# Two LoRA layers on one core: the first weight product fed chunk by chunk, and half of a small product moved into the weight stage

## The chip, the core and the metric

The kernel runs on one core of a Trainium2 chip. The metric is the device time of one execution in microseconds (us). Before the change the median of three runs is 326.9 us (325.46 to 327.69).

## What is computed

Two residual layers follow one another, each with a dense weight and a low-rank part that an index per batch picks:

```python
# layer 0: x is 8 x 256 x 1024, W0 1024 x 1024, rank 32, scale 16/32
x = x + einsum('bsi,oi->bso', x, W0) + (einsum(x, lora_A0[idx0[b]]) @ lora_B0.T) * 0.5
# layer 1: W1 1024 x 1024, bias b, rank 16, scale 2
x = x + einsum('bti,oi->bto', x, W1) + b + (einsum(x, lora_A1[idx1[b]]) @ lora_B1[idx1[b]]) * 2
```

All in 32-bit floats. The residual is the identity added to the weight, so the dense part is x (I + W0)^T (I + W1)^T. The kernel multiplies the two weights first, into one matrix M, and then x by M.

## The kernel before

The engines are TensorE (PE), VectorE (DVE), ScalarE (ACT), GpSimd (POOL) and SyncE (SP), which issues most DMAs. The order of the work on each engine is the order of the program text, written out by hand (`manual_schedule`, L937); each engine runs its own instructions in that order and waits for the others by semaphores. DMAs of the hardware queues take turns on eight semaphores, so a DMA is issued only when the one eight before it has landed.

There are two stages. The weight stage (to about 115 us) forms M from W0 and W1 in halves of 512 columns and rows, by a scheme with seven block products in place of eight, at two levels. The x stage then takes the batches in four pairs. The change lies in the first 55 us of the weight stage:

- Loads (L943 to L956). `w1_rows` holds W1's first 256 rows, in two DMAs on SP and ACT. Then SP loads W0's chunks k = 0 to 3 of the first column half (`load_w0`, L173; 128 x 512, 256 KB each), the second half of W1's first block (`load_w1`, L163, four DMAs of 128 KB), the block W1[0,1] (four of 256 KB), W0's chunks 4 to 7, the small `b0`, and W1[1,0] and W1[1,1].
- Warm-up and turning (L960 to L986). PE multiplies the identity by itself, then turns the eight 128 x 128 squares of `w1_rows` into two PSUM banks. One DVE and one ACT copy bring them to `w1T` (L1021, L1022).
- First products (L1023 to L1032, `first`). The first block product P1 has four groups of rows, each in a PSUM bank of its own, and four chunks k. The columns 0 to 255 come first, with the identity added to W0 (`diag_w0`, L180) and to W1 (L1030) by DVE.
- Then `turn_w1` (L225) turns the other half of W1's first block on DVE, 32 x 32 squares at a time, and the columns 256 to 511 follow, group by group; ACT keeps each group's result (`keep_p1`, L294) and puts it back into PSUM as the start of other sums (`load_inner`).
- `load_a1` (L193) fetches the eight picked rank-16 matrices A1 by eight DMAs of 64 KB on POOL. A POOL copy from `m22` (L195) holds them until the first group is kept. POOL then copies each to its place in `a1` (L203).
- Four turnings of W1[0,1] on DVE; then the "second" block product (class `Second`, L609), which is itself a seven-product scheme: `products([1, 2])` for its two halves, then, after the sums of W1's quarters on DVE (`Second.op.sums`, L416 to L421), products 6, 5, 4, 7, 3 of each.
- `prepare_up` and `prepare_down` (L716, L744): small products for the low-rank parts. `prepare_down(h)` is half h of G = A1 times (I + W0): eight products of 128 x 512 over all eight chunks of W0's column half h, and one ACT copy. Before, both halves stand behind the second block product, after `prepare_up(h)`.
- Beside it DVE turns W1[1,0], adds up the second product (`form`, L584), turns W1[1,1], forms the sums of W1's blocks (`sums_w1_first`, L354; four calls of two) with the four `diag_w0` of chunks 4 to 7 among them, and the sums of W0 (`w_groups[0].sums`, L264). POOL adds the identity to W1[1,*] (L235). The product of L282 that follows ("product 6" of the first group) needs all of these but W0's last two sums.

Of the kernel before, what the change touches and what calls it, by code (L numbers as in the profile page):

```python
# [10 lines left out]
ALU = mybir.AluOpType  # L11
# [9 lines left out]
P = 128  # L21
# [3 lines left out]
MLOW = 64  # L25
BIAS = 48
NWARM = 6
# [6 lines left out]
NQ = NH // 2  # L34
NB = 4
# [6 lines left out]
def kernel(  # L42
# [37 lines left out]
    nc = tc.nc  # L80

    B, T, D = x.shape
    NJ = T // P
    NK = D // P
    NO = D // NH
    NR = NH // SQ
    N0, _, R0 = lora_a0.shape
    N1, _, R1 = lora_a1.shape
# [5 lines left out]
    ident = const.tile([P, P], F32, tag="ident", name="ident")  # L94
# [34 lines left out]
    def fix_indices(rawi, n: int, layer: int):  # L129
        wrap = const.tile([1, B], I32, tag=f"wrap{layer}", name=f"wrap{layer}")  # L130
        nc.vector.tensor_scalar(wrap, rawi, 0, n, ALU.is_lt, ALU.mult)
        fixed = const.tile([1, B], I32, tag=f"fixed{layer}", name=f"fixed{layer}")
        nc.vector.tensor_tensor(fixed, rawi, wrap, ALU.add)
        nc.vector.tensor_scalar(fixed, fixed, 0, n - 1, ALU.max, ALU.min)
        return fixed

    def index(fixed, b: int, n: int, engine=SP):
        return nc.values_load(
            fixed[0:1, b : b + 1],
            engines=[engine],  # L140
            min_val=0,
            max_val=n - 1,
            skip_runtime_bounds_check_because="clamped on the chip",
        )
# [14 lines left out]
    def new_w1(h: int, i: int):  # L159
        both = units[:, 4 * h + 2 * i : 4 * h + 2 * i + 2].rearrange("p u n -> p (u n)")  # L160
        return both.rearrange("p (t c) -> p t c", t=NR)

    def load_w1(wq, h: int, i: int, lo: int = 0, hi: int = NR):  # L163

        rows = slice(h * NH + lo * SQ, h * NH + hi * SQ)
        for g in range(NG):
            cols = slice(i * NH + g * P, i * NH + (g + 1) * P)
            nc.sync.dma_start(  # L168
                wq[g * SQ : (g + 1) * SQ, lo:hi, :],
                w1[rows, cols].rearrange("(t q) c -> q t c", q=SQ),  # L170
            )

    def load_w0(k: int, i: int):  # L173
        cols = slice(i * NH, (i + 1) * NH)
        rows = w0[(k // NB) * NH : (k // NB + 1) * NH, cols]
        nc.sync.dma_start(
            w0n[:, k, cols], rows.rearrange("(p m) c -> p m c", m=NB)[:, k % NB, :]
        )

    def diag_w0(k: int):  # L180
        diag = w0n[:, k].rearrange("p (i q m) -> p i m q", i=2, m=NB)[:, k // NB, k % NB]
        nc.vector.tensor_tensor(diag, diag, ident, ALU.add)

    def load_b0():
        nc.sync.dma_start(
            b0.rearrange("p (i m) r -> p i (m r)", i=2),
            lora_b0.rearrange("(i p m) r -> p i (m r)", i=2, m=NB),
        )
# [2 lines left out]
    a1_rows = work[:, 0 : 2 * NH].rearrange("p (b k r) -> p b k r", b=B, k=NK)  # L191

    def load_a1():  # L193

        nc.gpsimd.tensor_copy(a1_rows[0:1, 0, 0, 0:1], m22[0:1, 0, 0:1])  # L195
        for b in range(B):
            j = index(fixed1, b, N1, mybir.EngineType.Pool)
            nc.gpsimd.dma_start(
                a1_rows[:, b].rearrange("p (i m) r -> p i (m r)", m=NB),
                lora_a1[bass.ds(j, 1)].rearrange("o (i p m) r -> p (o i) (m r)", i=2, m=NB),  # L200
            )
        for b in range(B):
            nc.gpsimd.tensor_copy(a1[:, :, b, :], a1_rows[:, b])  # L203
# [45 lines left out]
    def new_bank():  # L249
        ring.append(ring.pop(0))  # L250
        return ring[-1]
# [102 lines left out]
    def sums_w1_first(k: int):  # L354
        nc.vector.tensor_tensor(tw[:, 1, k, :], w_b["22"](k), w1T[:, k, NH:D], ALU.subtract)
        nc.vector.tensor_tensor(tw[:, 0, k, :], tw[:, 1, k, :], w_b["11"](k), ALU.add)
# [277 lines left out]
    def load_inner(ps, tiles):  # L634

        p = m22[:, tiles, :].rearrange("p m (h n) -> p (m h) n", h=2)
        for i, part in ((2, 0), (4, 2), (5, 3)):
            nc.scalar.copy(slot(ps, i), p[:, part])
# [77 lines left out]
    def prepare_up(h: int):  # L716
        pm = new_bank()
        for k in range(NK):
            g = k % 4
            nc.tensor.matmul(  # L720
                pm[g * R0 : (g + 1) * R0, :],
                b0[:, k, :],
                w1T[:, k, h * NH : (h + 1) * NH],
                start=(k < 4),
                stop=(k >= NK - 4),
            )
        nc.scalar.copy(ups[1][:, h * NH : (h + 1) * NH], pm)
# [13 lines left out]

    gT = [work[:, (4 + h) * NH : (5 + h) * NH] for h in range(NO)]

    def prepare_down(h: int):  # L744
        pm = new_bank()
        for k in range(NK):
            nc.tensor.matmul(  # L747
                pm,
                a1[:, k].rearrange("p b r -> p (b r)"),
                w0n[:, k, h * NH : (h + 1) * NH],  # L750
                start=(k == 0),
                stop=(k == NK - 1),
            )
        nc.scalar.copy(gT[h], pm)
# [182 lines left out]
    with tc.manual_schedule(engines=ORDERED):  # L937
# [5 lines left out]
        w1_rows = units[:, 0].rearrange("p (t c) -> p t c", t=2)  # L943
        for t, engine in enumerate((nc.sync, nc.scalar)):
            engine.dma_start(w1_rows[:, t], w1[t * P : (t + 1) * P, 0:NH])
        for k in range(NB):
            load_w0(k, 0)
        load_w1(wq[0, 0], 0, 0, mid, NR)
        wq[0, 1] = new_w1(0, 1)
        load_w1(wq[0, 1], 0, 1)  # L950
        for k in range(NB, NK):
            load_w0(k, 0)
        load_b0()
        for i in range(2):
            wq[1, i] = new_w1(1, i)
            load_w1(wq[1, i], 1, i)  # L956
        nc.scalar.copy(s_all[:, 0:R0], ident[:, 0:R0])


        def warm_up(first, last):  # L960
            for n in range(first, last):
                bank, i = banks[6 + n // 4], n % 4
                nc.tensor.matmul(
                    bank[:, i * P : (i + 1) * P],
                    ident,
                    ident,
                    start=(i == 0),
                    stop=True,
                    skip_group_check=True,
                )  # L970

        warm_up(0, NWARM)
        w1_turned = [banks[4 + t].rearrange("p (m q) -> p m q", m=NB) for t in range(2)]
        for t in range(2):
            for m in range(NB):
                rows = w1_rows[:, t].rearrange("p (q m) -> p m q", m=NB)[:, m]
                nc.tensor.matmul(
                    w1_turned[t][:, m, :],
                    rows,
                    ident,  # L980
                    start=(m == 0),
                    stop=True,
                    is_transpose=True,
                    skip_group_check=True,
                )
        warm_up(4, 7)  # L986
        raw0, raw1 = load_indices(idx0, 0), load_indices(idx1, 1)
        nc.gpsimd.memset(scale, L1_SCALING)
        for half in range(2):
# [20 lines left out]
        def first(g, k: int, n: int):  # L1010
            cols = slice(n * NH // 2, (n + 1) * NH // 2)
            nc.tensor.matmul(  # L1012
                g.p1[:, cols],
                g.a[0][:, k, :],
                w1T[:, k, cols],
                start=False,
                stop=(k == NB - 1),
                skip_group_check=True,
            )

        nc.scalar.copy(w1T[:, 0:NB, P : 2 * P], w1_turned[1])  # L1021
        nc.vector.tensor_copy(w1T[:, 0:NB, 0:P], w1_turned[0])  # L1022
        for k in range(NB):  # L1023
            diag_w0(k)
            if k == 0:

                part = w1T[0:MLOW, 0, 0:1]
                diag = bass.AP(part.tensor, part.offset, [part.ap[0], [D + 1, NB], [NB, MLOW]])
                same = ident[0:MLOW, 0:MLOW].unsqueeze(1).to_broadcast([MLOW, NB, MLOW])
                nc.vector.tensor_tensor(diag, diag, same, ALU.add)  # L1030
            for g in w_groups:
                first(g, k, 0)  # L1032
        fixed0, fixed1 = fix_indices(raw0, N0, 0), fix_indices(raw1, N1, 1)
        for k in range(NB):
            turn_w1(wq[0, 0], 0, k, mid, NR)
        seconds = [Second(n) for n in range(2)]
        one, other = seconds
        zero_inner(one.ps)
        for m, g in enumerate(w_groups):
            for k in range(NB):  # L1040
                first(g, k, 1)
            g.keep_p1(m22[:, m, :])
            if m % 2:
                load_inner(seconds[m // 2].ps, seconds[m // 2].tiles)
        load_a1()
        for k in range(NB, NK):
            turn_w1(wq[0, 1], 0, k)
        one.products([1, 2])
# [12 lines left out]
        other.products([6, 5, 4, 7, 3])  # L1061
        keep(other.kept, other.ps)
        prepare_up(0)
        prepare_down(0)
        for k in range(NB):
            turn_w1(wq[1, 0], 1, k)
        one.form()
        for k in range(NB):
            turn_w1(wq[1, 1], 1, NB + k)
        for k in range(NB):  # L1070
            sums_w1_first(k)
            if k == 1:
                for n in range(NB, NK):
                    diag_w0(n)
        prepare_up(1)
        prepare_down(1)
        prepare_cross()
        w_groups[0].sums()
        sums_w1_last()
# [280 lines left out]
```

## Time and profile before

| What | us |
| --- | --- |
| median of three runs | 326.9 |
| the profiled execution | 325.97 |
| its span, first to last instruction | 323.9 |
| PE busy in the span | 317.9 (98%) |
| DVE busy in the span | 253.7 (78%) |
| PE's first product on weights | at 7.05 |
| PE's chain without gaps begins | at 15.77 |

The span is cut into stretches by the steps above. The columns are the busy time of each engine with its number of instructions, the granted clock of PE (1.00 is full), the mean share of the DMA engines' time (over 1 where packets overlap) and the rate.

```profile
0.00:7.05 7.05, 4.84 (x26) 4.54 (x26) 3.66 (x8) 2.09 (x3) 5.15 (x22) 1.00 0.68 230
7.05:15.77 8.72, 8.48 (x38) 7.34 (x39) 5.40 (x18) 0.00 (x0) 0.00 (x0) 1.00 1.22 187
15.77:24.99 9.22, 9.22 (x42) 8.08 (x43) 7.32 (x13) 4.12 (x10) 5.26 (x9) 1.00 1.17 219
24.99:34.00 9.01, 9.01 (x46) 7.72 (x48) 8.94 (x17) 1.84 (x4) 3.20 (x7) 1.00 1.19 174
34.00:53.02 19.02, 19.02 (x80) 7.18 (x80) 15.08 (x24) 4.06 (x8) 3.13 (x6) 1.00 0.70 174
53.02:120.00 66.98, 66.98 (x250) 42.91 (x247) 60.98 (x111) 14.89 (x31) 26.49 (x30) 1.00 0.73 127
```

In a line of a timeline the first number is the start, the second the time covered, then engine, source line, operation, tiles, count, and in brackets the idle time before it and what ended it. In the chain of waits a line is start, length and what the time went to.

### The profile page before, as it was taken

What the parts mean: (1) busy time and instruction counts of PE and PEld (TensorE: products, weight loads), DVE (VectorE), ACT (ScalarE), POOL (GpSimd) and SP (SyncE); (2) the same over time, 40 slices, a digit from 0 to 9 for tenths busy, and PEclk for the clock granted to TensorE, in tenths of its full rate; (3) what the DMA queues carried; (4) which work ended last, traced back from release to release, by engine and by line L of the source; (5) the groups of instructions that cost most, each with busy time, mean ns of one, the idle gap of its engine ahead of it and who ended that gap; (6) DMA issues with size and microseconds to landing.
All of it is one profiled execution on the core that took longest, in us unless ns stands there. A gap on an engine that the chain in (4) does not pass through costs nothing.

```text
span 323.9 us, 4417 instructions
## 1 busy us (share of the span) xinstructions
PE 317.9 (98%) x1494; PEld 247.0 (76%) x1494; DVE 253.7 (78%) x490; ACT 59.9 (18%) x125; POOL 70.1 (22%) x107
## 2 busy tenths in 40 slices
PE   7999999999999999999999999999999999999995
PEld 6888434444588878888878888878888878888884
DVE  5679599879999899999969686929775929632965
ACT  2052215000224223640010420000240000222000
POOL 6053232455132231671004000003100000000000
PEclk9999999999999999999999999999999999999999
DMA  7999954987264995796417610235630111100113
GB/s 223 188 227 171 267 127 78 170 139 152 56 100 85 193 165 95 112 172 108 129 68 187 153 34 0 92 104 146 156 74 0 65 67 65 65 2 0 66 67 130
DMA packets 64910, 36.42 MB, mean 112 GB/s; under 512 B 45508, under 2 KB 58932, under 8 KB 64888
## 3 DMA queue, kind: packets, MB, share of 16 engines
q1 hardware_dynamic: 56088, 20.87, 29.7%
q0 software_dynamic: 8656, 15.01, 22.5%
q8 instruction: 12, 0.20, 0.2%
q10 hardware_dynamic: 144, 0.26, 0.2%
q14 instruction: 10, 0.08, 0.1%
HBM read 19.02 MB, written 8.39 MB: 85 GB/s over the span
## 4 chain that ended last, share of the span: by engine, by line
PE 94%; DMA 3%; DVE 1%; issue 0%; SPq 0%; DVEq 0%
PE bank L527 71%; PE bank L282 11%; PE bank L797 4%; PE bank L747 4%; DMA units<-in_L_cond_W_dram 3%; PE bank L1012 2%; PE bank L720 1%; DVE w1T L227 1%; PE bank L815 1%; DVE w1T L235 0%; PE bank L761 0%; PE bank L547 0%; DVE work L885 0%; SPq L168 0%; DVEq L227 0%
## 5 line engine op out<-in xcount | busy, mean ns | idle before, releaser
L509 DVE TENSOR_TENSOR work<-bank,work 128x512 f32<-128x512 f32 (+1 forms) x56 | 32.1, 618 | 30.6 <-PE bank L527 15.4
L505 ACT COPY work<-bank 128x512 f32<-128x512 f32 (+1 forms) x60 | 27.6, 546 | 77.3 <-PE bank L527 52.2
L931 POOL DMA_DIRECT2D out_dram<-work x12 | 8.9, 743 | 115.8 <-DVE work L607 115.8
L240 DVE STREAM_TRANSPOSE units<-units 128x512 f32<-128x512 f32 x32 | 20.1, 680 | 6.8 <-DMA units<-in_x_dram 6.8
L527 PE MATMUL bank<-w0n,w1T 128*128 128x256 f32 x104 | 24.1, 379 | 0.0
L527 PE MATMUL bank<-w1T,s_all 128*128 128x256 f32 x88 | 22.3, 379 | 0.0
L527 PEld LDWEIGHTS bank<-w0n,w1T 128*128 128x128 f32 x104 | 19.8, 190 | 2.7
L527 PE MATMUL bank<-w0n,m 128*128 128x256 f32 x88 | 20.9, 380 | 0.0
L227 DVE STREAM_TRANSPOSE w1T<-units 128x512 f32<-128x512 f32 (+1 forms) x16 | 14.9, 984 | 6.9 <-DMA w0n<-in_L_cond_W_dram 3.7
L527 PEld LDWEIGHTS bank<-w0n,m 128*128 128x128 f32 x88 | 16.6, 190 | 2.6 <-issue 0.4
L527 PEld LDWEIGHTS bank<-w1T,s_all 128*128 128x128 f32 x88 | 16.7, 190 | 2.3
L527 PE MATMUL bank<-tw,m 128*128 128x256 f32 x68 | 16.8, 379 | 0.0
L527 PE MATMUL bank<-tw,s_all 128*128 128x256 f32 x64 | 16.1, 379 | 0.0
L805 ACT ACTIVATE a<-bank,shift,scale 128x256 f32<-128x256 f32 x4 | 2.3, 564 | 72.4 <-PE bank L797 72.4
L1012 PE MATMUL bank<-w1T,w0n 128*128 128x256 f32 x64 | 14.4, 382 | 0.9 <-DVE w1T L1030 0.7
L527 PE MATMUL bank<-m,units 128*128 128x256 f32 x64 | 15.1, 379 | 0.0
L797 PE MATMUL bank<-units,down 128*64 128x256 f32 x128 | 14.7, 382 | 0.0
L1012 PEld LDWEIGHTS bank<-w1T,w0n 128*128 128x128 f32 x64 | 12.4, 196 | 2.7 <-DVE w1T L1030 0.9
L527 PE MATMUL bank<-w0n,s_all 128*128 128x256 f32 x56 | 14.4, 379 | 0.0
L747 PE MATMUL bank<-w0n,a 128*128 128x512 f32 x32 | 14.3, 599 | 0.0
L527 PEld LDWEIGHTS bank<-tw,m 128*128 128x128 f32 x68 | 12.9, 190 | 1.8
L282 PE MATMUL bank<-tw,s_all 128*128 128x512 f32 x32 | 14.2, 595 | 0.0
(263 smaller groups left out, 662.1 us busy)
## 6 DMA issues: line engine op xcount, KB each, us to landing
units<-in_x_dram SPq DMA_DIRECT2D x128, 64.0 KB, 2.4
out_dram<-work POOLq DMA_DIRECT2D x12, 512.0 KB, 3.5
w0n<-in_L_cond_W_dram SPq DMA_DIRECT2D x16, 256.0 KB, 7.7
units<-in_L_cond_W_dram SPq DMA_DIRECT2D x13, 256.0 KB, 8.7
out_dram<-work SPq DMA_DIRECT2D x3, 512.0 KB, 2.8
down<-in_L_cond_lora_A_dram SPq DMA_DIRECT2D x32, 32.0 KB, 2.6
w1T<-m POOLq DMA_DIRECT2D x4, 256.0 KB, 5.3
s_all<-units POOLq DMA_DIRECT2D x2, 512.0 KB, 5.3
```

The costliest lines, as they stand in the source:

```text
L227: nc.vector.transpose(w1T[:, k, cols].rearrange("p (t q) -> p t q", q=SQ), wq[:, lo:hi].rearrange("p t (q m) -> p m t q", m=NB)[:, k % NB],)
L240: nc.vector.transpose(xT[:, NX * j : NX * (j + 1), :].rearrange("p c (t q) -> p c t q", q=SQ), xq[:, :, j, :].rearrange("p t (q c) -> p c ...
L282: nc.tensor.matmul(pm, a[:, k, :], b(k), start=first and k == 0, stop=(k == NB - 1), skip_group_check=not first,)
L505: nc.scalar.copy(at_home(v, n), whole(ps, n))
L509: nc.vector.tensor_tensor(at_home(v, n), whole(ps, n), at_home(v, n), ALU.add)
L527: nc.tensor.matmul(slot(ps, i) if dst is None else dst, lhs, rhs, start=BANK[i][0] not in started, stop=stop, skip_group_check=True,)
L720: nc.tensor.matmul(pm[g * R0 : (g + 1) * R0, :], b0[:, k, :], w1T[:, k, h * NH : (h + 1) * NH], start=(k < 4), stop=(k >= NK - 4),)
L747: nc.tensor.matmul(pm, a1[:, k].rearrange("p b r -> p (b r)"), w0n[:, k, h * NH : (h + 1) * NH], start=(k == 0), stop=(k == NK - 1),)
L797: nc.tensor.matmul(pl[n * MLOW : (n + 1) * MLOW, :], downs[n][:, k, :], x_b[f"{n + 1}{k // NB + 1}"][:, k % NB, :], start=(k == 0), stop=( ...
L815: nc.tensor.matmul(pl, join, low, start=True, stop=True, skip_group_check=True)
L931: eng.dma_start(out[b, :, h * NH : (h + 1) * NH].rearrange("(j p) d -> p j d", p=P), ob[:, 0:D].rearrange("p (j d) -> p j d", d=NH),)
L1012: nc.tensor.matmul(g.p1[:, cols], g.a[0][:, k, :], w1T[:, k, cols], start=False, stop=(k == NB - 1), skip_group_check=True,)
```

## The change

W1's first rows are turned chunk by chunk: one chunk's two squares into a bank of its own, copied at once by DVE (chunk 0) or ACT (the others), its diagonal added for that chunk alone, and the products of chunk k start before the later chunks are turned. W0's chunks 2 and 3 are loaded behind W1's half block. Chunks 4 to 7 come ahead of W1[0,1] and are held by a one-row DVE memset until chunk 1 is on its way. Three warm-up products go. A1's loads are issued in the same place, six from ACT and two from POOL, without the copy that held them. The columns 256 to 511 of the first product run chunks first, groups 2 and 3 finished first. Half 0 of G follows directly, in the bank of group 3, ahead of the four turnings of W1[0,1]. On DVE the four `diag_w0` of chunks 4 to 7 move between the second and third turning of W1[1,1], and half 1 of G comes before `prepare_up(1)`.

```diff
     def load_a1():
-        nc.gpsimd.tensor_copy(a1_rows[0:1, 0, 0, 0:1], m22[0:1, 0, 0:1])
         for b in range(B):
-            j = index(fixed1, b, N1, mybir.EngineType.Pool)
-            nc.gpsimd.dma_start(
+            engine = nc.scalar if b < 6 else nc.gpsimd
+            j = index(fixed1, b, N1, engine.engine)
+            engine.dma_start(
...
-    def prepare_down(h: int):
-        pm = new_bank()
+    def prepare_down(h: int, pm):
...
-        for k in range(NB):
+        for k in range(2):
             load_w0(k, 0)
         load_w1(wq[0, 0], 0, 0, mid, NR)
-        wq[0, 1] = new_w1(0, 1)
-        load_w1(wq[0, 1], 0, 1)
-        for k in range(NB, NK):
+        for k in range(2, NB):
             load_w0(k, 0)
...
+        def turn_first(m: int):
+            for t in range(2):
+                nc.tensor.matmul(
+                    banks[4 + m][:, t * P : (t + 1) * P],
+                    w1_rows[:, t].rearrange("p (q m) -> p m q", m=NB)[:, m],
                     ident,
...
+            copy = nc.scalar.copy if m else nc.vector.tensor_copy
+            copy(w1T[:, m, 0:NQ], banks[4 + m][:, 0:NQ])
+
+        def diag_first(m: int):
+            diag = w1T[0:MLOW, m, 0:NQ].rearrange("p (q m) -> p m q", m=NB)[:, m]
+            nc.vector.tensor_tensor(diag, diag, ident[0:MLOW, 0:MLOW], ALU.add)
...
+        for m in range(2):
+            turn_first(m)
+            diag_first(m)
+            if m == 0:
+                diag_w0(0)
+        fixed0 = fixed1 = None
         for k in range(NB):
+            if k + 2 < NB:
+                turn_first(k + 2)
+                diag_first(k + 2)
+            if k:
+                diag_w0(k)
+            if k == 1:
+                fixed1, fixed0 = fix_indices(raw1, N1, 1), fix_indices(raw0, N0, 0)
+                nc.vector.memset(w0n[0:1, NB:NK, 0:1], 0.0)
+            for g in sorted(w_groups, key=lambda g: g.m % 2 == k % 2):
                 first(g, k, 0)
+        for k in range(NB, NK):
+            load_w0(k, 0)
+        load_a1()
+        wq[0, 1] = new_w1(0, 1)
+        load_w1(wq[0, 1], 0, 1)
+        load_b0()
...
-        for m, g in enumerate(w_groups):
-            for k in range(NB):
+        for k in range(NB // 2):
+            for g in w_groups:
                 first(g, k, 1)
-            g.keep_p1(m22[:, m, :])
-            if m % 2:
-                load_inner(seconds[m // 2].ps, seconds[m // 2].tiles)
-        load_a1()
+        for both in (slice(2, 4), slice(0, 2)):
+            for k in range(NB // 2, NB):
+                for g in w_groups[both]:
+                    first(g, k, 1)
+            for g in w_groups[both]:
+                g.keep_p1(m22[:, g.m, :])
+        for s in seconds:
+            load_inner(s.ps, s.tiles)
+        prepare_down(0, banks[3])
         for k in range(NB, NK):
             turn_w1(wq[0, 1], 0, k)
...
         prepare_up(0)
-        prepare_down(0)
         for k in range(NB):
             turn_w1(wq[1, 0], 1, k)
         one.form()
         for k in range(NB):
             turn_w1(wq[1, 1], 1, NB + k)
-        for k in range(NB):
-            sums_w1_first(k)
             if k == 1:
                 for n in range(NB, NK):
                     diag_w0(n)
+        for k in range(NB):
+            sums_w1_first(k)
+        prepare_down(1, new_bank())
         prepare_up(1)
-        prepare_down(1)
         prepare_cross()
```

## The prediction

> **What bounds the kernel now.** I read the page's busy times and its chain first, then the chain in order of time for the first 60 us, then VectorE's (DVE's) timeline from 17 to 53 us, and last the landings of single weight loads.
>
> ```profile
> PE 317.9 (98%) x1494; PEld 247.0 (76%) x1494; DVE 253.7 (78%) x490; ACT 59.9 (18%) x125; POOL 70.1 (22%) x107
> ```
> ```profile
> 4.77 6.98 DMA units<-in_L_cond_W_dram
> ...
> 15.77 5.88 PE bank L1012 x26
> 21.66 12.34 PE bank L527 x56
> 34.00 1.85 PE bank L720 x16
> 35.85 7.06 PE bank L747 x16
> 42.92 2.54 PE bank L720 x16
> 45.45 7.06 PE bank L747 x16
> 52.52 0.57 PE bank L761 x16
> 53.09 7.06 PE bank L282 x16
> ```
> TensorE (PE) is the bound from 15.77 us to the end; before that the chain is W1's load, landed at 11.75. Hence only two things can move the time: when PE starts and stands still in the first 16 us, and whether a wait appears later in this gapless row. The two 7.06 are G's halves; the first one is moved. The first product after this part (L282) begins at 53.0.
>
> ```profile
> 18.09 4.13 DVE L227 STREAM_TRANSPOSE w1T<-units 128x512 f32<-128x512 f32 x4 [1.77 <-DMA units<-in_L_cond_W_dram]
> ...
> 24.20 0.69 DVE L419 TENSOR_TENSOR s_all<-s_all,w1T 128x512 f32<-128x512 f32 x1
> ...
> 28.91 4.11 DVE L227 STREAM_TRANSPOSE w1T<-units 128x512 f32<-128x512 f32 x4
> ...
> 35.04 0.51 DVE L607 TENSOR_TENSOR m<-units 128x256 f32<-128x256 f32 x1
> 39.28 4.11 DVE L227 STREAM_TRANSPOSE w1T<-units 128x512 f32<-128x512 f32 x4 [3.73 <-DMA w0n<-in_L_cond_W_dram]
> ...
> 46.15 1.26 DVE L182 TENSOR_TENSOR w0n<-w0n,ident 128x128 f32<-128x128 f32 x4
> ...
> 50.69 0.69 DVE L269 TENSOR_TENSOR s_all<-s_all,w0n 128x512 f32<-128x512 f32 x1
> ```
> This is a second chain beside PE's. It starts when W1[0,1] has landed (18.0), and ends when the sum of L269 is ready (51.4), without which the product at 53.0 can't start. In all that time DVE rests only 3.73 us, and is just 1.6 us ahead of PE at the end. So DVE has 5.4 us of room against PE in this stretch, while 7.06 us of PE's work is taken out of it.
>
> ```profile
> L176 SPq DMA_DIRECT2D w0n<-in_L_cond_W_dram x1: 328/328/328, 39.1 to 39.1; - x1
> ...
> DMA to landing us min/median/max: 6.7/6.7/6.7
> ```
> The last of the eight loads of W0's second column half is issued at 39.1 and lands at 45.8. Before, DVE adds the identity to it (L182) at 46.15, so nothing waits.
>
> **The change part by part.** Times are the profiled execution's (325.97 us, span 323.9), which is 0.9 below the median 326.9.
>
> *Start.* The rows land at 4.40. Eight turnings took 1.4 us, so two take some 0.35; then a DVE copy of 128x256 (0.42, as L483) and a 64x64 sum (0.27, L235) stand before the first product instead of a 128x512 copy (0.69), a 128x128 sum (0.41) and a 64x256 sum (0.65). First product at 5.6 instead of 7.05. The three extra diagonal sums (3 x 0.27), three ACT copies (some 0.35 each) and three warm-up products fewer (0.1 to 0.2 us each) lie beside PE's products.
>
> *First half of the products.* W1's half (4 loads) now comes ahead of W0's chunks 2 and 3. The first 2 MB ended at 11.75 whatever its order, so chunk 3 lands at about 11.75, where it landed at 9.3. PE has used up chunks 0 to 2 by then and waits; this takes back most of the earlier start. After 11.75 come 4 + 16 products of 0.43 us (64 records took 2 x 0.216 each): 20.4 instead of 21.5. DVE's four turnings of W1's half (0.65 + 0.27 each, 12.2 to 16.1) stay ahead of them. Worth 1.1 us to PE here.
>
> *A1 early.* The copy of L195 (0.18) and its wait for the first kept product go. Six loads go to ACT's queue, two stay on POOL's; the index is fixed at about 9.2 (DVE's six small operations took 1.0). By the new order of the semaphores the fifth and sixth of ACT's loads wait until W0's chunks 4 and 5 have landed (13 to 14.5), and ACT's four keeping copies stand behind them; the first is needed at about 18.7, so this costs nothing unless chunk 5 lands over 4 us late. POOL's eight copies (0.3 to 0.9) have no one else behind them until 40. An A1 load is 64 KB in 256-byte pieces like x's, which land after 2.8 us on ACT's kind of queue; through POOL under full load they took 8.3 to 10.8. So the last load, issued at 14.5, lands between 17.3 and 25.3, and G can start soon after that, its copy included. I take 20.4, PE's own time, since six of eight go the way of x's loads.
>
> The Trainium skill, "DMA: Bandwidth & Descriptors", Specifications, speaks against this: it puts the least transfer for full rate at 512 bytes, with a read-modify-write below. By it A1's 0.5 MB would cost as much as 1 MB of W1, an estimated 6.2 us instead of the 2.6 below, and the sum would be 3.6 us worse.
>
> *W1[0,1] behind W0's chunks 4 to 7.* SP holds these, and with them all of W1's later loads that stand behind in its queue, until a tiny DVE memset (about 9.8); the DMAs ahead run until 11.75, so no queue runs dry. Before, the same 4 MB had landed at 21.4 (12.4 + 9.0, the last W0 chunk). Now A1 is in it as well: between 0 and 3.1 us (half of the 6.2 us that W1's 1 MB took). I take 2.6: W1[0,1] lands at 24.0, 6 us later than before. DVE's chain starts there.
>
> *G's half.* 7.06 us from 20.4 to 27.5, plus one ACT copy (0.59) beside it. It covers the wait for W1[0,1]; the same 7.06 go away between 35.85 and 42.92. Then four products, and four more that need two DVE sums and a memset behind the turnings (24.0 + 4.13 + 1.14 = 29.3): PE reaches "product 6" (24.99 before) at 31.0. From there to L282 it needs 28.0 - 7.06 = 21.0: PE is ready at **52.0**, 1.0 earlier than 53.0.
>
> *DVE's chain, the step that decides.* From the landing of W1[0,1] to the second sum (18.0 to 24.9) 6.9; from there to L269's end 26.5, of which 3.73 was waiting: 22.8 of work. 24.0 + 6.9 + 22.8 = **53.7**. The change also puts the four diagonal sums between the second and the third of W1[1,1]'s turnings. The last of them needs the load that landed at 45.8; behind it DVE has 0.35 + two turnings (2.06) + eight sums (5.6) + two sums (1.4) = 9.1 or a little more overlapped, from the rows 8.8 + 0.35: 45.8 + 9.1 = **54.9**. What that landing does is the open term: A1's way may spare or cost the queues some 1 us, a load that lands 1.2 us earlier would leave DVE's own work to decide (53.7), W1's rate for A1 (3.1 us) instead of what POOL's took would bring it up to some 56. I take 54.9, as every byte ahead of that load is also ahead of it before. PE waits 2.9 us before L282, for DVE.
>
> *After it.* DVE had 1.3 and 2.2 us of rest at 62 and 65 us, so its lag is gone by then, and PE carries the shift to the end.
>
> **Sum.** L282 at 54.9 instead of 53.0: +1.9 us. 325.97 + 1.9 = 327.9 for a profiled execution, 326.9 + 1.9 = **328.8** as a median.
>
> The granted clock is 1.00 in every stretch before, and no wait of PE after the first 5 us is over 0.9 us. The Trainium skill, "TensorE: Matmul & The Clock Gate", "Why this matters for your kernels", asks for no gap over some 3 us, or the array runs at half clock: by it the 2.9 us are at the edge, and an estimated 1.7 us (half of a window of 3.4) would come on top. I leave it out.
>
> **Rivals.**
> *A1 comes late (slower).* POOL's copies wait for the last A1 load as in the trace (10.8 us after issue): G starts at 25.3 or later. DVE's wait hides a start up to 23.3; after that each us costs one. PE would be ready at 52.0 + 4.9 = 56.9: +3.9, 330.8. For it: DMA share 1.17 to 1.22, so all queues are full; against it: x's loads.
> *DVE isn't late.* The weights land early enough: W0's last load by 42.9 and W1[0,1] by 22.3. Then PE's 52.0 holds: -1.0, 325.9. For it: the transfers lagged at 46 while the DMA share fell to 0.70 on average after 34; against it: A1's bytes now come before both.
> *DVE's work alone decides.* The last load lands by 44.5: L282 at 53.7, +0.7, 327.6.
> *The early start does nothing:* PE's gain of 1.1 in the first part is covered by the wait anyway; the time stays 328.8, within the forecast.
>
> **How the numbers follow.** A measurement of this kernel tells about 1% (3.3 us) from no change; its three runs spread 0.7%. Forecast (DVE behind the late load) 0.6, own range 327.8 to 330; DVE's work alone 0.15; DVE not late 0.1; A1 late 0.15. The range leaves out half of the third and somewhat over half of the last: 326.3 to 331.0. Faster by over 1% would need more than PE's later start (1.45) and its three waits up to 36 us (0.6, 0.4, 0.8) together: 0.03. Slower by over 1% (330.2) is most of A1 late and little of the forecast: 0.16. Within 1%: 0.81.
>
> **What would show it.** PE's first product near 5.6; a wait of PE near 11 for W0; G's first half (L745 in the new numbering) at 20 to 23 without a wait on POOL; L226's turning of W1[0,1] at about 24; DVE's L182 waiting for W0 near 45; PE idle 2 to 3 us before the first product of that line (L281 there), released by DVE. Wrong if that idle time is under 1 us or G waits for A1 beyond 23.3.

## The result and the profile after

The changed kernel takes 328.09 us (median of 22 runs, 326.1 to 329.32), the kernel before 325.31 on the same chips (22 runs, 324.3 to 327.69). The ratio is 1.0073, interval 1.0059 to 1.0088: slower by 0.7%, which is within 1%. The forecast was 328.8 with 326.3 to 331.0. The profiled execution of after took 329.05 us with a span of 327.4; that of before 325.97 with 323.9. The span is 3.5 us longer.

Line numbers have shifted: the product that was L282 is now L281, G is L745, A1's load and copy L197 and L202, W1's turning L226, the first product L1007, the memset that holds W0's chunks L1031.

The busy times of after, from its page:

```profile
PE 318.3 (97%) x1488; PEld 246.8 (75%) x1488; DVE 253.3 (77%) x494; ACT 60.0 (18%) x127; POOL 66.7 (20%) x100
```
Nothing was added to any engine that would carry 3.5 us. The time must be rest or a changed order, so the timeline of PE in after comes next:

```profile
5.96 2.00 PE L1007 MATMUL bank<-w1T,w0n 128*128 128x256 f32 x8 [0.41 <-DVE w1T L980]
...
9.25 11.50 PE L1007 MATMUL bank<-w1T,w0n 128*128 128x256 f32 x52 [0.19 <-DVE wrap L131]
21.49 7.13 PE L745 MATMUL bank<-w0n,a 128*128 128x512 f32 x16 [0.74 <-POOL a L202]
...
54.80 5.37 PE L281 MATMUL bank<-tw,s_all 128*128 128x512 f32 x8 [2.57 <-DVE s_all L268]
```
PE starts earlier (5.96 instead of 7.05) and its first product ends at 9.25 + 11.50 = 20.75 without waiting for W0. G follows at 21.49. In the last line lies the loss: 2.57 us of rest, and a product that starts at 54.80 where before it started at 53.02. That is 1.78 us of the 3.5.

The rest is the clock. The stretches of after around that product (columns as before; the granted clock is the number after POOL's):

```profile
54.00:56.00 2.00, 1.20 (x3) 0.68 (x4) 2.00 (x4) 0.25 (x1) 2.00 (x2) 0.99 0.31 50
56.00:59.30 3.30, 3.30 (x5) 1.33 (x4) 3.30 (x6) 1.94 (x4) 1.21 (x3) 0.50 1.17 182
```
PE is busy for the whole 3.3 us at a granted clock of 0.50: it does half the work of that time, so 1.7 us go. The chain of waits shows the same: the 80 products from L281 on took 36.27 us in after and 34.53 before.

```profile
54.80 36.27 PE bank L281 x80
```
and before:

```profile
53.09 34.53 PE bank L282 x80
```
1.78 + 1.74 = 3.5, the whole difference of the spans. The half clock begins near 56, a good 1 us after the rest has ended; from 59.4 to 62 the clock is 1.00 again.

It is not in every execution. Of after's 22 runs, 11 have a mean clock of 0.995, as the profiled one has (median 328.54), and 11 have 1.0 (median 326.79): 1.75 us apart. At full clock after is 326.79 - 325.31 = 1.5 us slower than before, and the half clock in half of the runs makes up the other 1.3 us of the median. Two of after's full-clock runs (328.72 and 328.79), and seven of 29 runs of before with a clock of 0.999 or more (326.5 to 327.8, median of the 29 325.06), lie some 2 us above the others, so something besides the half clock moves a run by that much, and what it is stays open.

The profiled execution is one of the slowest of after. At full clock it would have taken an estimated 329.05 - 1.74 = 327.3, and the median of the full-clock runs is 0.5 below that. So the 2.57 us of rest are this execution's; in the others it was probably shorter.

What made DVE late is in its timeline in after. It rests for the last time before 25.19:

```profile
10.03 0.06 DVE L1031 MEMSET w0n<- 1x4 f32 x1
...
25.19 4.04 DVE L226 STREAM_TRANSPOSE w1T<-units 128x512 f32<-128x512 f32 x4 [10.12 <-DMA units<-in_L_cond_W_dram]
...
44.34 1.51 DVE L182 TENSOR_TENSOR w0n<-w0n,ident 128x128 f32<-128x128 f32 x4
...
53.96 0.69 DVE L268 TENSOR_TENSOR s_all<-s_all,w0n 128x512 f32<-128x512 f32 x1
```
L182 has no bracket: W0's last load landed at 43.72 and nothing waited for it, where the forecast had it land at 45.8 and decide. DVE works without a rest from 25.19 to the sum that PE waits for. So what matters in this execution is when W1[0,1] lands (25.07; 17.96 before), and the chain of waits of after says what that depended on:

```profile
11.30 5.44 DMA work<-in_L_cond_lora_As_dram
16.75 0.33 SPq L168
17.13 0.49 SPq L168
17.66 7.41 DMA units<-in_L_cond_W_dram
```
SP could issue the second of W1[0,1]'s four loads only when one of A1's had landed, at 16.74: the DMAs of ACT and SP take turns on the same eight semaphores. The last one, out at 17.7, needed 7.4 us. The landing varies from execution to execution: e1_fill, e2_form_late and e8_gap are the same kernel up to there, and in their profiles W1[0,1]'s turning starts at 24.20, 24.61 and 23.76.

### The profile page after: what moved, and what is told of

Read it like the earlier page. It is cut to its first block, busy times and chain, and to the rows that moved or that the text cites. A ratio compares the mean times of both kernels' runs of the same rounds, so it can differ in the third digit from the quotient of the medians.

```text
span 327.4 us, 4402 instructions
## 1 busy us (share of the span) xinstructions
PE 318.3 (97%) x1488; PEld 246.8 (75%) x1488; DVE 253.3 (77%) x494; ACT 60.0 (18%) x127; POOL 66.7 (20%) x100
## 4 chain that ended last, share of the span: by engine, by line
PE 83%; DMA 7%; DVE 6%; issue 1%; SPq 1%; ACTq 0%; ACT 0%; DVEq 0%
PE bank L526 66%; PE bank L281 11%; PE bank L795 4%; DMA units<-in_L_cond_W_dram 3%; DVE w1T L226 2%; DMA work<-in_L_cond_lora_As_dram 2%; DMA w0n<-in_L_cond_W_dram 1%; DVE s_all L482 1%; DMA down<-in_L_cond_lora_A_dram 1%; SPq L207 1%; PE bank L1007 1%; PE bank L813 1%; DVE w0n L182 1%; PE bank L966 0%; SPq L168 0%
## 5 line engine op out<-in xcount | busy, mean ns | idle before, releaser
L226 DVE STREAM_TRANSPOSE w1T<-units 128x512 f32<-128x512 f32 (+1 forms) x16 | 15.0, 982 | 10.2 <-DMA units<-in_L_cond_W_dram 10.1
L281 PE MATMUL bank<-tw,s_all 128*128 128x512 f32 x32 | 15.8, 653 | 2.6 <-DVE s_all L268 2.6
L1007 PE MATMUL bank<-w1T,w0n 128*128 128x256 f32 x64 | 14.5, 383 | 0.6 <-DVE w1T L980 0.4
L745 PE MATMUL bank<-w0n,a 128*128 128x512 f32 x32 | 14.3, 599 | 0.7 <-POOL a L202 0.7
L281 PEld LDWEIGHTS bank<-tw,s_all 128*128 128x128 f32 x32 | 6.6, 208 | 11.1 <-issue 8.1
```

The source lines that it names most:

```text
L226: nc.vector.transpose(w1T[:, k, cols].rearrange("p (t q) -> p t q", q=SQ), wq[:, lo:hi].rearrange("p t (q m) -> p m t q", m=NB)[:, k % NB],)
L281: nc.tensor.matmul(pm, a[:, k, :], b(k), start=first and k == 0, stop=(k == NB - 1), skip_group_check=not first,)
L745: nc.tensor.matmul(pm, a1[:, k].rearrange("p b r -> p (b r)"), w0n[:, k, h * NH : (h + 1) * NH], start=(k == 0), stop=(k == NK - 1),)
L1007: nc.tensor.matmul(g.p1[:, cols], g.a[0][:, k, :], w1T[:, k, cols], start=False, stop=(k == NB - 1), skip_group_check=True,)
```

## The experiments

Theory A, after these traces: the loss is DVE's lateness, set by W1[0,1]'s landing, and a half clock that the rest of PE brings with it; G's move itself costs nothing. What stands against it is named in each expectation as theory B. Each run is compared with the kernel before on its own chip (325.28 us of 35 runs for e1 to e4, 325.06 of 29 for e5 to e8). The ratio and its interval are those on record. They are not the quotient of the two medians, which is 0.001 to 0.003 higher in every row (1.0062 for e6_g_only, 0.9988 for e5_both), so a difference of 0.3% between two rows says little by itself; the traces carry the argument.

| Run | what differs | us | ratio to before, interval | L281 starts at | PE's rest before it |
| --- | --- | --- | --- | --- | --- |
| after | | 328.09 | 1.0073, 1.0059 to 1.0088 | 54.80 | 2.57 |
| e1_fill | 8 filler products in the rest | 326.32 | 1.0016, 0.9991 to 1.0042 | 53.82 | filled |
| e8_gap | 3 filler products | 326.58 | 1.0027, 1.0006 to 1.0049 | 53.24 | 0.96 |
| e2_form_late | `form` behind the sums | 324.95 | 0.9969, 0.9945 to 0.9993 | 52.57 | 0.86 |
| e3_no_hold | no memset | 325.57 | 0.9992, 0.9968 to 1.0015 | 53.09 | 1.40 |
| e5_both | e2 and e3 together | 324.67 | 0.9965, 0.9941 to 0.999 | 51.17 | none |
| e4_start_only | the early start alone | 324.29 | 0.9961, 0.9936 to 0.9987 | 51.64 | none |
| e6_g_only | without early start and hold | 327.07 | 1.0033, 1.0008 to 1.0059 | 55.38 | 1.26 |
| e7_a1_pool | all of A1 from POOL | 334.24 | 1.0253, 1.0218 to 1.0289 | 61.43 | 1.39 |

**e1_fill: is the half clock a term of its own?** The fillers multiply the identity by itself into a free bank; nobody uses what they give.

```diff
         prepare_cross()
+        for n in range(8):
+            nc.tensor.matmul(
+                banks[7][:, 0:P], ident, ident, start=True, stop=True, skip_group_check=True
+            )
```

> The changed kernel with eight products identity by identity (128x128, unused result) put on TensorE between the small cross product and the product of line 281 that waits for VectorE. Theory A (the wait of 2.6 us for VectorE costs 1.8, and the half clock of 3.4 us that follows it in part of the runs costs 1.7 more): the product still starts at 54.8, but no stretch has half clock, the runs stop falling into two heaps, median 326.8, ratio to before 1.0045. Theory B (the half clock has nothing to do with the wait, or costs nothing): the median stays at 328.1, ratio 1.0085, with the dip still there. The fillers could also delay the product: then it starts after 55.0 and the time is 328 or more with full clock.

Measured: 326.32 us, and none of its runs has a clock under 0.998. PE in e1_fill:

```profile
51.93 2.05 PE L1093 MATMUL bank<-ident 128*128 128x128 f32 x16 [0.51 <-ACT cross L766]
```
PE multiplies the fillers instead of resting. The real product starts at 53.82, still later than before's 53.02, but the runs near 328.5 are gone. The median is 1.8 us below after's. Part of this need not be the clock: in this run's profile W1[0,1] happened to be 1 us earlier (its turning starts at 24.20). Beside after's runs at full clock (326.79) it is 0.5 lower.

**e8_gap: how long may the rest be?** Three fillers instead of eight, their results unused as well.

```diff
+        for n in range(3):
+            nc.tensor.matmul(
+                banks[7][:, 0:P], ident, ident, start=True, stop=True, skip_group_check=True
+            )
```

> The changed kernel with three fillers instead of eight ahead of the product of line 281, so that TensorE rests about 1.9 us behind them instead of 2.6. Theory A (the half clock comes when enough of one stretch of 3.4 us is idle): seldom or never half clock, median 326.4 as with eight fillers, ratio 1.003. Theory B (any rest of TensorE over 1 us can bring it): half clock in about half of the runs, median 327.5 to 328, ratio 1.007.

Measured: 326.58 us, no clock under 0.998 in its 12 runs. In the profile the fillers are followed by 0.96 us of rest. That is less than was wanted, since here DVE was earlier than in after (its turning of W1[0,1] starts at 23.76). So a rest of about 1 us costs itself only; where between 1 and 2.57 us the half clock begins isn't told by this run. Both fillers support theory A: together 24 runs without a half clock, against 11 of 22 with one in after.

**e2_form_late: is DVE's work what ends last?** DVE's adding up of the second product, `form` (some 2.5 us that no one needs before L281), goes behind the sums. Nothing else changes.

```diff
         for k in range(NB):
             turn_w1(wq[1, 0], 1, k)
-        one.form()
         for k in range(NB):
             turn_w1(wq[1, 1], 1, NB + k)
...
         w_groups[0].sums()
+        one.form()
```

> The changed kernel with the five VectorE sums that add up the second product's first half (2.5 us) put behind the sums of W0 instead of ahead of W1[1,1]'s turnings. Theory A (VectorE's own work ends last before the product of line 281): the sum that it waits for ends at about 53.0 instead of 54.7 (2.5 earlier, less about 0.7 of waiting for W0's last chunk, which landed at 43.7), TensorE waits 0.8 us, no half clock, median 325.4, ratio 1.000. Theory B (the loads end last, VectorE only waits for them): the product stays at 54.8, median 328.1, ratio 1.0085.

Measured: 324.95 us, ratio 0.9969 (0.9945 to 0.9993). DVE and PE in e2_form_late:

```profile
43.23 0.40 DVE L182 TENSOR_TENSOR w0n<-w0n,ident 128x128 f32<-128x128 f32 x1 [0.39 <-DMA w0n<-in_L_cond_W_dram]
```
```profile
52.57 7.11 PE L281 MATMUL bank<-tw,s_all 128*128 128x512 f32 x16 [0.86 <-DVE s_all L268]
```
L281 comes 2.2 us earlier, and no run has a clock under 0.998. Some 0.6 of that is W1[0,1], whose turning starts at 24.61 instead of 25.19. The other 1.6 is the edit: from that turning to the end of the sum that PE waits for (L268) DVE needs 27.8 us instead of 29.5. W0's last load, which the forecast had decide, costs 0.39 us here, now that DVE reaches it 2 us earlier. So DVE's work was what ended last, as theory A has it.

**e3_no_hold: what does the memset do?**

```diff
                 fixed1, fixed0 = fix_indices(raw1, N1, 1), fix_indices(raw0, N0, 0)
-                nc.vector.memset(w0n[0:1, NB:NK, 0:1], 0.0)
```

> The changed kernel without the tiny VectorE memset that holds W0's chunks 4 to 7 until 10.1 us. Theory A (the hold left the DMA engines half idle from 9.5 to 12 us, and W1[0,1] landed that much later, at 25.1): W1[0,1] lands at 23.0 to 23.5, VectorE's chain begins and ends 1.6 to 2 us earlier, the product of line 281 starts at 53.0, median 325.5, ratio 1.0005. Theory B (W1[0,1] waits for A1's loads, whose landing frees the issue of its four DMAs): it lands at 25 as with the hold, median 328.1, ratio 1.0085; W0's chunk 3 lands at 11.7 instead of 10.1 in both.

Measured: 325.57 us, ratio 0.9992 (0.9968 to 1.0015). One line is worth 2.6 us (0.0081 of 325.3), with the half clock that goes as well. The stretches of after:

```profile
8.00:12.00 4.00, 3.81 (x19) 3.15 (x18) 3.16 (x14) 0.37 (x1) 0.89 (x2) 1.00 0.56 163
12.00:16.00 4.00, 4.00 (x20) 3.65 (x19) 2.85 (x8) 0.00 (x0) 0.89 (x2) 1.00 1.03 315
16.00:21.00 5.00, 4.75 (x23) 3.97 (x21) 0.00 (x0) 1.72 (x4) 1.50 (x6) 1.00 1.24 159
```
and the same stretches of e3_no_hold:

```profile
8.00:12.00 4.00, 3.81 (x19) 3.14 (x18) 3.20 (x13) 0.37 (x1) 0.93 (x2) 1.00 1.05 370
12.00:16.00 4.00, 4.00 (x20) 3.65 (x19) 2.85 (x8) 0.00 (x0) 0.58 (x1) 1.00 1.27 192
16.00:21.00 5.00, 4.72 (x22) 3.94 (x21) 0.00 (x0) 1.75 (x4) 2.03 (x8) 1.00 1.26 197
```
PE's work is the same in both. The last two columns differ: with the hold the DMA engines are busy for 0.56 of 8 to 12 us, without it for 1.05. Until 21 us after has moved 4 x 163 + 4 x 315 + 5 x 159 = 2707 KB, e3_no_hold 4 x 370 + 4 x 192 + 5 x 197 = 3233 KB. The 526 KB that after is behind are some 3 us at 159 to 197 GB/s; W1[0,1]'s turning starts at 25.19 in after and 21.77 in e3_no_hold, 3.4 apart. The order of the issues has its part: without the hold two of W1[0,1]'s four loads are out by 10.3, before the first of A1's (10.32); with it one is out at 13.7 and three only from 16.75 on. W0's chunk 3 landed at 10.28 without the hold and at 10.11 with it; the expectation on that was missed, as the hold does nothing to it.

But L281 starts only 1.7 us earlier than in after (53.09), and PE still rests 1.40. DVE's timeline in e3_no_hold shows where the remainder went:

```profile
38.08 0.42 DVE L600 TENSOR_TENSOR units<-units 128x256 f32<-128x256 f32 x1 [1.57 <-ACT units L504]
```
This is `form`. It adds up the second product's first half, which ACT brings out of PSUM, and with G moved ahead of it PE makes that product some 7 us later than before. DVE, now early, stands 1.57 us for it, about the 1.40 that PE stands later. So W1[0,1]'s landing is one thing that makes DVE late, and G's move, by way of `form`, is another. The time is that of theory A, but in part by luck: the landing came 1.4 us earlier than theory A had it, and the wait before `form` took as much back.

**e5_both: is anything left of the loss?** The edits of e2 and e3 together.

```diff
-                nc.vector.memset(w0n[0:1, NB:NK, 0:1], 0.0)
...
-        one.form()
...
         w_groups[0].sums()
+        one.form()
```

> The changed kernel without the hold and with the five sums of the second product put late: both things taken away that made VectorE late. Theory A (the whole loss is VectorE's lateness, and the move of G is otherwise neutral): no wait of TensorE before the product of line 281, which starts at 51.6 as in the run with the new start alone; median 324.3, ratio 0.997. Theory B (the move of G costs TensorE something by itself, through A1's late arrival or the loads): the product starts at 52.5 or later, ratio 0.999 or more.

Measured: 324.67 us, ratio 0.9965 (0.9941 to 0.999). L281 starts at 51.17, and the bracket that would name a rest is missing:

```profile
51.17 7.13 PE L281 MATMUL bank<-tw,s_all 128*128 128x512 f32 x16
```
With G moved, A1 early and no rest, the change gains 0.35% by the ratio on record and 0.1% by the medians (324.67 against 325.06). Theory A holds: the loss of after was DVE's lateness. The move of G costs PE nothing here, where the hold is gone and `form` no longer stands in DVE's way; with `form` in its old place it still cost the 1.40 us of e3_no_hold.

**e4_start_only: does the early start matter without the rest?** W1's first rows chunk by chunk, and W0's chunks 2 and 3 behind W1's half block. Everything else is as before: A1's loads with their copy, W1[0,1] ahead of W0's chunks 4 to 7, both halves of G behind the second product. Against after, cut:

```diff
+        nc.gpsimd.tensor_copy(a1_rows[0:1, 0, 0, 0:1], m22[0:1, 0, 0:1])
...
-                nc.vector.memset(w0n[0:1, NB:NK, 0:1], 0.0)
...
-        prepare_down(0, banks[3])
...
+        prepare_down(0, new_bank())
```

> Only the first part of the change: W1's first rows turned, completed and multiplied chunk by chunk, with W0's chunks 2 and 3 behind W1's half block; A1, G, the order of all later loads and of VectorE's sums as in the kernel before. Theory A (VectorE's chain from W1[0,1]'s landing at 18.0 sets the product 6 of the second product at 24.9 whatever TensorE has done earlier): TensorE begins at 6 instead of 7, ends the first product about 1 us earlier, waits that much longer, and the median is that of before, ratio 0.999 to 1.001. Theory B (TensorE's own work sets the end of this stage): 0.9 us faster, ratio 0.997.

Measured: 324.29 us, ratio 0.9961 (0.9936 to 0.9987). Theory A, that it gains nothing, fell. The chain of waits of e4_start_only:

```profile
9.31 5.89 PE bank L1007 x26
...
15.24 5.88 PE bank L1007 x26
21.12 12.17 PE bank L526 x56
...
51.71 12.64 PE bank L281 x29
```
Before, PE's row without gaps began at 15.77; here it begins at 9.31, and nothing but PE is in the chain from there. W1's half block comes early enough for its turnings to stay ahead of PE. L281 starts 1.4 us earlier than before (51.64), and 1.0 of that is in the median. Theory A had counted on DVE's chain starting at 18.0, and that did not hold either: the turning of W1[0,1] starts at 16.52 instead of 18.09. This is the part of the change that gains by itself, and the lowest median here, though e5_both and e2_form_late are not told apart from it by the intervals.

**e6_g_only: the rest of the change without that start.** The start of before, with the new order of loads, A1's loads early, G's half moved and the new order on DVE; no memset. Against after, cut:

```diff
-        for k in range(2):
+        for k in range(NB):
             load_w0(k, 0)
...
-        for k in range(2, NB):
-            load_w0(k, 0)
...
-        for m in range(2):
-            turn_first(m)
-            diag_first(m)
...
+        nc.scalar.copy(w1T[:, 0:NB, P : 2 * P], w1_turned[1])
+        nc.vector.tensor_copy(w1T[:, 0:NB, 0:P], w1_turned[0])
```

> The second part of the change alone: A1 early, W0's chunks 4 to 7 ahead of W1[0,1], G's first half after the first product, the new orders of VectorE and G; the start is that of the kernel before, and there is no hold. Theory A (moving G gains nothing, because TensorE has nothing to wait for in the kernel before once the weights flow; it only takes room from VectorE): TensorE reaches the product of line 281 at 53, VectorE at 51.5 to 53.5 with W1[0,1] landing at 21.5 to 22.5, ratio 0.999 to 1.003. Theory B (moving G is what loses the time, whatever the start and the hold): 2 us slower, ratio 1.006 or more.

Measured: 327.07 us, ratio 1.0033 (1.0008 to 1.0059). By the ratio this lies between the two theories, by the medians (2.0 us over 325.06) it is theory B, and the 12 runs spread from 325.35 to 328.01, so it decides neither. The profile is of the slowest of the twelve. PE in e6_g_only:

```profile
23.69 7.13 PE L745 MATMUL bank<-w0n,a 128*128 128x512 f32 x16 [2.12 <-POOL a L202]
```
G waits 2.12 us for A1, and W1[0,1]'s turning starts at 25.88, 4.1 later than in e3_no_hold, which differs from this kernel only in the start. W1[0,1]'s four loads go out from 10.95 to 19.22 us here and from 8.40 to 16.82 there. So the start also decides when the loads behind it are issued. Which of its two halves does that, the order of W0's and W1's loads or the earlier index for A1, was not tried. Where A1 comes late, as here, G's move does cost PE time. G's wait, and the 1.26 us before L281, brought no half clock: the clock is 0.998 or more in every run.

**e7_a1_pool: does the way by which A1 comes matter?** All eight loads from POOL, in the same place.

```diff
-            engine = nc.scalar if b < 6 else nc.gpsimd
+            engine = nc.gpsimd
```

> The changed kernel with all eight A1 loads issued by GpSimd at the same place, none by ScalarE. Theory A (with the six on ScalarE's queue, W1[0,1]'s DMAs are held by A1's landing, 16.7 us for the second of them; but A1's bytes are the same): W1[0,1] is issued earlier and lands at about 24, 1 us earlier, VectorE's chain with it; A1's eight loads go out 0.95 us apart from 10.9 on and land up to 8 us later, so G starts at 23 to 25 and not at 21.5, and TensorE's wait before the product of line 281 becomes a wait before G; median 327.5 to 328.5, ratio 1.007 to 1.010. Theory B (A1's route matters neither way): G at 21.5, ratio 1.0085.

Measured: 334.24 us, ratio 1.0253 (1.0218 to 1.0289), far beyond the expectation. PE in e7_a1_pool, and its stretches where the clock changes:

```profile
26.72 10.02 PE L745 MATMUL bank<-w0n,a 128*128 128x512 f32 x16 [5.88 <-POOL a L202]
```
```profile
24.00:25.70 1.70, 0.00 (x0) 0.00 (x0) 1.70 (x2) 0.00 (x0) 0.84 (x3) 1.00 1.22 177
25.80:32.50 6.70, 5.78 (x7) 2.53 (x8) 6.58 (x14) 0.00 (x0) 0.29 (x1) 0.50 1.23 201
```
POOL issues one load in about 0.93 us (the last at 17.62), and they land a median of 8.7 us after issue, against 5.4 for the six on ACT's queue and two on POOL's in after. G waits 5.88 us, and the half clock that the rest brings is twice as long as in after: it begins just under 1 us before the rest ends and goes on to 32.5, so G's 16 records take 10.02 us instead of 7.13. W1[0,1]'s loads go out earlier, as expected (the last at 13.6 instead of 17.7), but its turning starts at 23.98, no earlier than in the runs with after's loads (23.76 to 25.19), and it no longer helps: DVE stands 7.74 us before `form` (L600), for the second product that PE makes behind the late G. Without the six loads on ACT's queue the moved G would cost far more than it does.

## Why the prediction was right, and where it was not

The predicted time holds (328.8 against 328.09), the signs of the parts hold, and the step called decisive, DVE's sum ending after PE, is what happened to a tenth of a us: 54.8 against 54.9 for L281. But the reason given for 54.9 was not the one that held, so it was partly luck. Two of the signs named did not come: no wait of PE for W0 near 11, and no wait of L182 near 45.

- *PE's start.* 5.6 was forecast, 5.96 came. The first copy took the forecast 0.42; the turning of two squares took 0.59 instead of 0.35.
- *First product.* Its end was forecast at 20.4, it came at 20.75, for another reason. Chunk 3 landed at 10.11, not at 11.75 ("the first 2 MB ended at 11.75 whatever its order"), so PE never waited for W0; its own 52 products from 9.25 on set the end.
- *A1 and G.* G was forecast at 20.4 "without a wait on POOL"; it started at 21.49 after 0.74 us for POOL's last copies. A1's last load landed at 20.62, within the bounds 17.3 to 25.3. The rival *A1 comes late* did not occur here, but e7_a1_pool shows that it was a real one: with POOL's queue it costs 6 us more than after. The rule by which A1's 256-byte pieces would cost 3.6 us more did not come true: in e3_no_hold the turning of W1[0,1] starts at 21.77 although A1's loads are in the queues too (one is under way from 14.88 to 20.39 in its chain of waits), where the forecast had 21.4 for the same loads without A1.
- *"No queue runs dry".* This step failed. The memset was executed at 10.03, the chunks behind it were issued from 10.14, and the DMA engines were half idle from 8 to 12 us. It cost 3.4 us of W1[0,1]'s landing in this pair of profiles (2.0 to 2.8 against the three other runs with after's loads) and 2.6 us of time (e3_no_hold). The forecast landing, 24.0, came out near the measured 25.07 only since A1 had been charged with 2.6 us that the hold caused.
- *DVE's chain.* Its two lengths were right: 6.9 to the second sum and 22.8 after it. From the true landing they give 25.07 + 29.7 = 54.8, and L268 ended at 54.65. That is the rival *DVE's work alone decides* with a later start, and it was given 0.15. A second link was not in the prediction: `form` needs the second product, which G's move makes later, and e3_no_hold shows DVE standing 1.57 us for it.
- *The late load.* "What that landing does is the open term", and it was mis-sized: 43.72 instead of 45.8. No one waited for it in after, and 0.39 us in e2_form_late. The four terms behind it, 0.35 + 2.06 + 5.6 + 1.4, add up to 9.4 and not to the 9.1 that was used; from the last L182 to the end of L268 e2_form_late took 9.2.
- *PE's rest.* 2.9 forecast, 2.57 measured in the profiled execution. The three waits of 0.6, 0.4 and 0.8 us that the prediction counts to PE are those of its weight loads; PE's own row before has waits of 0.7 and 0.2 behind the warm-up.
- *The clock.* "I leave it out" was the second failed step. The Trainium skill, "TensorE: Matmul & The Clock Gate", "Why this matters for your kernels", asks for no rest over about 3 us, and its Part 1, "What's actually happening", tells of a window of 3413 ns that runs freely and does not start anew with the kernel. That such a window meets a rest in some runs and not in others is worked out from this, and fits the 11 of 22 runs. The trace agrees in the length (the clock record of after has half clock for 3.413 us) and in the price estimated by it (1.7; 1.75 between the medians at the two clocks). It differs in the threshold: in the profiled execution 2.57 us of rest was enough, and the measurement decides. On the median the half clock is 1.3 us (328.09 against 326.79).
- *The sum.* +1.9 was forecast for a median of 326.9; +2.78 came upon 325.31. The three runs shown had lain 1.6 high. The loss itself was 0.9 more than forecast: 1.3 by the clock left out, less 0.4 since at full clock it was 1.5 and not 1.9. The two errors, 1.6 and 0.9, point opposite ways, and 0.7 is left.
- *The rival "the early start does nothing"* fits after, where 2.57 us of rest swallow it. By itself the start does gain: 1.0 us in e4_start_only.

Why G's move does not help: it takes 7 us of PE's work out of the stretch in which DVE must catch up, and W1[0,1], DVE's first input, comes 7 us later than before. The second product, which `form` needs, comes some 7 us later as well. PE is done with its part at 54.80 - 2.57 = 52.2, 0.8 earlier than before, and then stands.

## What to carry to other kernels

When a block of the bound engine's work is moved to an earlier place, look at what another engine could do beside it in its old place: here it was the cover of DVE's chain, and taking 2.5 us of work that no one needed yet, and that waits for the delayed product, out of that chain was worth more than the move. A hold that keeps loads back should be laid beside the DMA share of the stretch before it is believed to be free. And in this kernel a rest of PE near 2.5 us is to be priced at its own length and, in part of the runs, 1.7 us for a half-clock stretch of 3.4 us.

## What was not expected of the hardware

- In the profiles a rest of PE of 2.57 us brought a half-clock stretch of 3.4 us, and one of 5.88 us a stretch twice as long; the six runs of that kernel have a clock of 0.985 to 0.99. Rests of 2.12, 1.40 and 0.96 us brought none.
- The clock changed in steps of one length. By the traces' clock records the half clock begins 51.20 us after the first record and lasts 3.413 us in after, and begins 20.48 us after it and lasts 6.827 us in e7_a1_pool: 15, 1, 6 and 2 times 3.413. Counted in such windows, PE idled 2.27 us of the one before the half clock in after, and the whole of it in e7_a1_pool. Windows at full clock with 1.49 us of idle time (e7_a1_pool) or less were followed by full clock. The 2.12 us of e6_g_only lie across a border, 1.33 and 0.79. So in these ten profiles it is the idle time within one window that goes with the half clock, and the least that brought it lies between 1.49 and 2.27 us of 3.413.
- An SP load waited for an ACT load to land: three of W1[0,1]'s loads were out only from 16.75 us on, when a load of A1 had landed at 16.74.
- The four later chunks of W0, issued from 10.1 to 11.5 us with A1's loads beside them, landed 3.3 to 5.1 us after their issue (315 GB/s from 12 to 16 us); W1[0,1]'s last load, as large, needed 7.4 us (159 to 183 GB/s from 16 to 28 us).
